# Small operations of the norms and of attention: other operands, other engines, and an identity added in four pieces

## The chip, the cores and the metric

The kernel runs on one core of one Trainium2 chip. The metric is the device time of one execution in microseconds (us). A core has five engines that each work through their own instructions in order: PE (TensorE, the matmuls; PEld is its weight load), DVE (VectorE), ACT (ScalarE), POOL (GpSimd) and SP (SyncE, here the queue that issues most DMAs). They wait for each other through semaphores only. SBUF is the large on-chip memory, PSUM the small one that the matmuls write.

## The reference, cut to what matters

Two layers work on x of shape (4, 512, 64, 64): 4 images of 512 channels and L = 4096 positions.

```
x = x + L0(gn(x))      # layer 0: layer norm, a Mamba scan over positions, layer norm, projection
x = x + L1(gn(x))      # layer 1: linear attention

gn(v): per image, 32 groups of 16 channels:  (v - mean) / sqrt(var + 1e-5)

L1:  q = relu(Wq x + bq);  k = relu(Wk x + bk);  v = Wv x + bv      # 8 heads of 64 channels
     kq   = sum over positions of k^T q                             # 64 x 64 a head
     attn = (v kq) / (kq.sum(axis=2) + 1e-6)
     out  = W_out attn + b_out
```

Three small pieces of this matter here. First, the statistics of `gn`: from the mean and the variance of each channel come the mean and the variance of each group, and from these a scale `gr` and an offset `off` for each channel. Secondly, kq is divided by its sum. Thirdly, layer 1 ends with `x + ...`, and the kernel folds that x into the last matrix by adding the identity to it.

## The kernel before, in words

Channels lie on partitions: 512 channels are NC = 4 blocks of P = 128. Positions are cut into NT = 8 tiles of T = 512. Layer 0 goes through 4 images x 8 tiles x 4 channel blocks = 128 steps (the list `steps`), each in SLOTS = 16 slots, so 2048 slots in all. In each slot the function `slot` issues

- on POOL, `drive`: one product `bx` of 128x1024 elements (L721), issued for the slot after next. `bx` has three buffers;
- on DVE, two scans `h` of 128x512 (L739), and in every second slot the product of `h` with `c_all` (L759, 128x1536);
- on ACT, two exponentials `dA` (L713) into three PSUM buffers, each released by a scan;
- on POOL, in every second slot, the copy `st` (L750) and the product of the last quarter of `h` with `c_sb` (L751);
- on PE, the matmuls that make `c_all` and those that sum `h` into `y`.

Then `slot` calls `after`, which issues everything else: the next steps' inputs, and the norms and layer 1 piece by piece. These pieces are Python generators in four queues: `ahead` (the norm of the next tile), `late` (the end of a tile in layer 0), `rest` (attention, that is layer 1) and `light` (the statistics of the next image). `one` takes one piece from a queue in a slot; whatever a generator issues between two `yield`s lies in that slot, behind the slot's scans on DVE. `later(1, f)` calls f in the next slot; `pause(1)` makes a generator go on in the next slot; `room` waits until few enough of the three PSUM work banks of `work_bank` are held, and `free` counts one back. So the order of each engine's instructions is written out by hand. Before the 2048 slots, and after them when only the attention of the last image is left, there are no slots (`now[0]` is None): `later` then calls at once, and `pause` does nothing.

The functions that the change touches:

- `stats_end` (L339 to L362) takes `mv`, the mean and variance of each channel (128x4 each), to `gr`, `off` and `ngm` (minus the group's mean). It copies the means to `cm` (L342), averages them over groups with a matmul with `grp` into the bank `pm`, copies that to `gm` (L347), forms the deviation and its square and adds the variance (L349 to L351), averages again (`pv`, in the same bank), adds the epsilon on DVE (L355), takes the power -1/2 on POOL (L357), and makes `ngm` and `off` on DVE (L360, L361). It runs twice an image: once for layer 0 (names ending in `_a`; from `input_norm`) and once for layer 1 (`_b`; from `attention`).
- `shifted` collects the sums for the second norm; for an image's first tile it takes a sample's statistics and sets `moff` (L554) and the first `square` (L556) on DVE.
- `shifted_end` (L567 to L576) turns these sums into `mv`: two reductions (L570), then on DVE a scaling (L571), `d2`, a subtraction and an addition (L573 to L575).
- `attention`, after kq is summed up: the reduction `nrm` (L898), + 1e-6 (L899), the reciprocal (L900), and two products of 64x256 into `kqn` (L903), which a POOL memset (L896) has zeroed. Then come the matmuls `pm` (twice), which fold the projections into one matrix `m3` (shown as `m` in the trace), and the matmuls `pob` for its offset `ob` (L951 on DVE). Last, 16 DVE additions of 32x32 (L976) put the identity onto `m3`'s diagonal, using `fold`, 32x32 identities stacked down the partitions. The matmuls `pr` then use `m3` for all 8 tiles, ACT adds `ob` (L979) and SP stores the result (L981).

All matmuls go through the helper `mm`, so every one of them has line L124.

Of the kernel before, what the change touches and what calls it, by code (L numbers as in the profile page):

```python
# [8 lines left out]
F32 = mybir.dt.float32  # L9
BF16 = mybir.dt.bfloat16  # L10
AF = mybir.ActivationFunctionType
ALU = mybir.AluOpType
AX = mybir.AxisListType

P = 128
T = 512
# [8 lines left out]
def kernel(  # L25
# [24 lines left out]
    nc = tc.nc  # L50
    B, C, L = x.shape
    NC = C // P
# [6 lines left out]
    BLK = 32  # L59
# [5 lines left out]
    small = ctx.enter_context(tc.tile_pool(name="small", bufs=2))  # L65
# [13 lines left out]
    def work_bank(name, behind=1):  # L79
        held[0] += behind  # L80
        return ps_w.tile([P, T], F32, tag="w", name=name)

    def free(n=1):
        held[0] -= n

    def later(n, what):

        done = []

        def both():  # L90
            what()
            done.append(True)

        if now[0] is None:
            both()
        else:
            due.append((now[0] + n, both))
        return done
# [5 lines left out]
    def until(*done):  # L104
        while not all(done):
            yield "wait"

    def pause(n):
        return until(later(n, lambda: None))

    def room(when="wait"):

        while now[0] is not None and held[0] >= limit[0]:
            yield when
# [6 lines left out]
    def mm(out_, lhsT, rhs, abreast=1, **how):  # L121

        work["mm"] += (0.25 if rhs.dtype == BF16 else 1.0) * rhs.shape[-1] / T / abreast
        nc.tensor.matmul(out_, lhsT, rhs, **how)  # L124
# [30 lines left out]
    def free_x():  # L155
        held_x[0] -= 1
# [17 lines left out]
    grp = const.tile([P, P // GROUP, GROUP], F32, tag="grp", name="grp")  # L174
# [9 lines left out]
    grp = grp.rearrange("p g i -> p (g i)")  # L184
# [4 lines left out]
    for i in range(1, 4):  # L189
        r = slice(i * LANE, (i + 1) * LANE)  # L190
# [10 lines left out]
    fold = const.tile([P, BLK], F32, tag="fold", name="fold")  # L201
    for k in range(KS):
        r = slice(k * BLK, (k + 1) * BLK)
# [47 lines left out]
    for e in range(NH):  # L251
        r = e * (LANE + NST)
# [30 lines left out]
    for i in (2, 3):  # L283
        r = slice(i * LANE, P)
# [16 lines left out]
    for o in range(NC):  # L301
        pw = work_bank(f"pw_{o}")
        for c in range(NC):
            mm(
                pw[:, 0:1], w_pr[:, c, o * P : (o + 1) * P], b_sb[:, c : c + 1],
                start=(c == 0), stop=(c == NC - 1),
# [13 lines left out]
    for c in range(NC):  # L320
        mm(
            pw[:, 0:1], ones.to_broadcast([P, P]), b_sb[:, c : c + 1],
            start=(c == 0), stop=(c == NC - 1),
# [8 lines left out]
    def aggregate(stats, name):  # L332

        mv = small.tile([P, NC, 2], F32, tag="mv", name=f"mv_{name}", bufs=4)
        for c in range(NC):
            nc.vector.bn_aggr(mv[:, c, :], stats[:, c, :, :].rearrange("p t s -> p (t s)"))
        return mv

    def stats_end(mv, name):  # L339

        cm = small.tile([P, NC], F32, tag="cm", name=f"cm_{name}")
        nc.vector.tensor_copy(cm, mv[:, :, 0])  # L342
        yield from room()
        pm = work_bank(f"pm_{name}")
        mm(pm[:, 0:NC], grp, cm, start=True, stop=True)
        gm = small.tile([P, NC], F32, tag="gm", name=f"gm_{name}")
        nc.vector.tensor_copy(gm, pm[:, 0:NC])  # L347
        dev = small.tile([P, NC], F32, tag="dev", name=f"dev_{name}")
        nc.vector.tensor_tensor(dev, cm, gm, ALU.subtract)  # L349
        nc.vector.tensor_tensor(dev, dev, dev, ALU.mult)  # L350
        nc.vector.tensor_tensor(dev, dev, mv[:, :, 1], ALU.add)  # L351
        pv = pm[:, NC : 2 * NC]
        mm(pv, grp, dev, start=True, stop=True)
        gr = small.tile([P, NC], F32, tag="gr", name=f"gr_{name}", bufs=4)
        nc.vector.tensor_scalar(gr, pv, 1e-5, None, ALU.add)  # L355
        free()
        nc.gpsimd.tensor_tensor(gr, gr, mhalf, ALU.pow)  # L357
        off = small.tile([P, NC], F32, tag="off", name=f"off_{name}", bufs=4)
        ngm = small.tile([P, NC], F32, tag="ngm", name=f"ngm_{name}", bufs=4)
        nc.vector.tensor_scalar(ngm, gm, -1.0, None, ALU.mult)  # L360
        nc.vector.tensor_tensor(off, ngm, gr, ALU.mult)  # L361
        return gr, off, ngm  # L362

    def group_norm(dst, xt, norm):
# [139 lines left out]
    def projected(ym, stats, x1, b, t):  # L504
# [27 lines left out]
        nc.gpsimd.dma_start(xt, cols(x, b)[:, :, t * T : (t + 1) * T], accum_op=ALU.add)  # L532
        yield from pause(4)
        yield from shifted(stats, xt, t, nm)
        nc.sync.dma_start(x1, xt)
        later(2, free_x)
# [9 lines left out]
    def shifted(f, xt, t, nm):  # L546
        if t == 0:
            for o in range(NC):
                nc.vector.bn_stats(f["first"][:, o, 0, :], xt[:, o, :])
                if o % 2:  # L550
                    yield
            f["mv"] = aggregate(f["first"], f"first_{nm}")
            f["off"] = small.tile([P, NC], F32, tag="moff", name=f"moff_{nm}")
            nc.vector.tensor_scalar(f["off"], f["mv"][:, :, 0], -1.0, None, ALU.mult)  # L554
            nc.vector.memset(f["sum"][:, :, 0:1], 0.0)
            nc.vector.tensor_scalar(f["square"][:, :, 0], f["mv"][:, :, 1], float(T), None, ALU.mult)  # L556
            return
        for o in range(NC):
            for v, func in (("sum", AF.Identity), ("square", AF.Square)):
                unused = wk.tile([P, T], F32, tag="res", name=f"{v}_{nm}_{o}", bufs=2)  # L560
                nc.scalar.activation(
                    unused, xt[:, o, :], func, bias=f["off"][:, o : o + 1],
                    accum_out=f[v][:, o, t : t + 1],
                )
            yield "free"

    def shifted_end(f, name):  # L567
        mv = small.tile([P, NC, 2], F32, tag="mv", name=f"mv_{name}", bufs=4)
        for v in range(2):
            nc.vector.tensor_reduce(mv[:, :, v], f[("sum", "square")[v]], AX.X, ALU.add)  # L570
        nc.vector.tensor_scalar(mv, mv, 1.0 / L, None, ALU.mult)  # L571
        d2 = small.tile([P, NC], F32, tag="d2", name=f"d2_{name}")
        nc.vector.tensor_tensor(d2, mv[:, :, 0], mv[:, :, 0], ALU.mult)  # L573
        nc.vector.tensor_tensor(mv[:, :, 1], mv[:, :, 1], d2, ALU.subtract)
        nc.vector.tensor_tensor(mv[:, :, 0], mv[:, :, 0], f["mv"][:, :, 0], ALU.add)  # L575
        return mv  # L576


# [227 lines left out]
    def attention(b, x1s, stats):  # L806
# [54 lines left out]
        for v in range(NT * SUB):  # L861
# [5 lines left out]
            for j in range(2):  # L867
# [4 lines left out]
                for c in range(NC):  # L872
                    mm(
                        pq, gn[:, c, u * P : (u + 1) * P], w_qk[:, c, j * C : (j + 1) * C],
                        start=False, stop=(c == NC - 1),
# [20 lines left out]
        nc.gpsimd.memset(kqn, 0.0)  # L896
        nrm = small.tile([P, NC], F32, tag="nrm", name=f"nrm_{b}")
        nc.vector.tensor_reduce(nrm, kq, AX.X, ALU.add)  # L898
        nc.vector.tensor_scalar(nrm, nrm, 1e-6, None, ALU.add)  # L899
        nc.vector.reciprocal(nrm, nrm)  # L900
        for i in range(P // HEAD):
            r = slice(i * HEAD, (i + 1) * HEAD)
            nc.vector.tensor_tensor(  # L903
                kqn[r, :, r], kq[r, :, :],
                nrm[r, :].unsqueeze(2).to_broadcast([HEAD, NC, HEAD]), ALU.mult,
            )
# [9 lines left out]
        for p in range(NC):  # L916
            yield from room()
            pm = work_bank(f"pm2_{b}_{p}")
# [6 lines left out]
        gr, _, ngm = norm  # L925
        m3 = wk.tile([P, NC, C], F32, tag="m3", name=f"m3_{b}", bufs=1)
# [6 lines left out]
        for m in range(NC):  # L933
            yield from room()
            pm = work_bank(f"pm3_{b}_{m}")
            for p in range(NC):
                mm(
                    pm, w_v[:, p, m * P : (m + 1) * P], m2[:, p, :],
                    start=(p == 0), stop=(p == NC - 1),
# [14 lines left out]
        for o in range(NC):  # L954
            yield from room()
            pm = work_bank(f"pob_{b}_{o}")
            for p in range(NC):
                mm(
                    pm[:, 0:1], m2[:, p, o * P : (o + 1) * P], bv[:, p : p + 1],
                    start=(p == 0), stop=False,  # L960
                )
            for m in range(NC):
                mm(
                    pm[:, 0:1], m3[:, m, o * P : (o + 1) * P], ngm[:, m : m + 1],
                    start=False, stop=(m == NC - 1),
# [3 lines left out]
        yield from until(*taken)  # L969
        free_x()  # L970
        free_x()
        for o in range(NC):
            for k in range(P // BLK):
                r = slice(k * BLK, (k + 1) * BLK)
                v = m3[r, o, o * P + k * BLK : o * P + (k + 1) * BLK]
                nc.vector.tensor_tensor(v, v, fold[r, :], ALU.add)  # L976
        def store(t, o, pp):
            res = wk.tile([P, T], F32, tag="res", name=f"res_{b}_{t}_{o}", bufs=2)
            nc.scalar.activation(res, pp, AF.Identity, bias=ob[:, o : o + 1])  # L979
            free()  # L980
            later(1, lambda: nc.sync.dma_start(cols(out, b)[:, o, t * T : (t + 1) * T], res))  # L981

        for t in range(NT):
            x1 = yield from fetched(t, "b")
            for o in range(NC):
                yield from room()
                pp = work_bank(f"pr_{b}_{t}_{o}")
                for m in range(NC):
                    mm(
                        pp, m3[:, m, o * P : (o + 1) * P], x1[:, m, :],  # L990
                        start=(m == 0), stop=(m == NC - 1),
# [39 lines left out]
    def leave(b, t):  # L1031
        if t == 0:
            stats1[b] = shifted_stats(b)
            x1s[b] = [
                dram.tile([P, NC, T], F32, tag="x1", name=f"x1_{b}_{i}", bufs=3 * NT)
                for i in range(NT)
            ]
        ym = xn[b, t][:, :, NTAP - 1 : NTAP - 1 + T]
        yield from projected(ym, stats1[b], x1s[b][t], b, t)
        if t == NT - 1:  # L1040
            add_to(rest, attention(b, x1s[b], stats1[b]))
# [52 lines left out]
    with tc.manual_schedule():  # L1094
        credit, seen, mix, held[0], held_x[0] = 0.0, work["mm"], iter(()), 0, 0
        for n, (b, t, c) in enumerate(steps):
            f, nm = fs[n], names[n]
# [142 lines left out]
```

## Time and profile before

| | us |
|---|---|
| median of 3 runs (lowest, highest) | 7940.75 (7933.85, 7962.12) |
| the profiled execution's own time | 7963.09 |
| its span, first to last instruction | 7961.4 |
| busy: DVE | 6977.7 (88% of the span) |
| busy: POOL | 6880.5 (86%) |
| busy: PE | 6453.6 (81%) |
| busy: ACT | 5507.6 (69%) |
| granted TensorE clock, mean | 0.897 |

Three stretches can be told apart by the busy time of the engines. Up to about 130 us the kernel sets up and takes the first statistics. From there to about 7400 us run most of the slots. From about 7500 us on only the attention of the fourth image is left: in the 461 us from 7500 to 7961, PE is busy for 425.2 us, DVE for 23.0 and POOL for 2.9.

A row of the groups of instructions gives the line, the engine, the operation, output<-inputs by the program's names, the shapes, and the count; then the busy time in us and the mean of one in ns; then the idle time of the engine just before these instructions in us, with what ended it. A line of the timeline gives start and duration in us, engine, line and operation, and in brackets the idle time before it with its releaser. The chain of waits is followed backwards from the last instruction: each of its pieces is a stretch of time which the end of the program waited for.

### The profile page before, as it was taken

To read this page: it belongs to the slowest core of one execution; us is meant where nothing else is said; L and a number is where in the kernel's file an instruction comes from. 1 tells how busy PE (TensorE), PEld (TensorE's weight loads), DVE (VectorE), ACT (ScalarE), POOL (GpSimd) and SP (SyncE) were. 2 spreads that over 40 slices of the span, in tenths; PEclk is the share of its full clock that TensorE was granted. 3 is DMA by queue.
4 is the path that set the end of the run, shared out by engine and by line. 5 is a ranking of instruction groups with operands and counts; after the bars stand their busy time and mean duration, and the time that the engine had idled before them with its cause. 6 is when DMAs were issued, how large, how long until landed. Compare 5 with 4: busy or idle time off the path is not lost.

```text
span 7961.4 us, 90563 instructions
## 1 busy us (share of the span) xinstructions
PE 6453.6 (81%) x24835; PEld 2120.0 (27%) x24880; DVE 6977.7 (88%) x5766; ACT 5507.6 (69%) x8321; POOL 6880.5 (86%) x4597
## 2 busy tenths in 40 slices
PE   5676777677789888888788888898688888888599
PEld 1121212112223222322222223332122332322144
DVE  5999999999999999989999999998999999988600
ACT  4667777777777777767777777677777777777421
POOL 4999999999999899989999899898999999889600
PEclk7888888888899999998899999899899999999799
DMA  5666666666666666777766666677666666676402
GB/s 154 167 168 166 151 155 159 160 155 167 169 179 162 151 163 159 174 189 175 174 155 171 171 157 161 155 185 189 156 167 163 161 161 159 145 194 180 112 32 90
DMA packets 829184, 1265.87 MB, mean 159 GB/s; under 512 B 183912, under 2 KB 317560, under 8 KB 816384
## 3 DMA queue, kind: packets, MB, share of 16 engines
q1 hardware_dynamic: 804736, 1222.32, 61.1%
q0 software_dynamic: 16896, 33.56, 2.4%
q10 hardware_dynamic: 7040, 4.20, 0.2%
q8 instruction: 195, 3.19, 0.2%
q14 instruction: 317, 2.60, 0.1%
HBM read 1052.78 MB, written 206.57 MB: 158 GB/s over the span
## 4 chain that ended last, share of the span: by engine, by line
DVE 33%; PE 21%; ACT 15%; DMA 12%; issue 8%; SPq 6%; POOL 6%; POOLq 0%; ACTq 0%; DVEq 0%
DVE h L739 22%; DVE h L759 9%; DMA d_all<-d_rows 7%; ACT dA L713 5%; PE pq L124 5%; POOL bx L721 4%; PE pc L124 4%; SPq L688 3%; PE y L124 3%; PE pr L124 3%; SPq L639 2%; DMA c_sb<-c_rows 2%; ACT xz L1048 2%; PE po L124 2%; ACT L1048 1%
## 5 line engine op out<-in xcount | busy, mean ns | idle before, releaser
L721 POOL TENSOR_TENSOR bx<-d_all,b_all 128x1024 f32<-128x1024 f32 x2048 | 4824.7, 2367 | 213.3 <-DVE h L739 195.1
L739 DVE TENSOR_TENSOR_SCAN h<-dA,st,bx 128x512 f32<-128x512 f32 x3584 | 4358.9, 1264 | 358.7 <-ACT dA L713 159.0
L713 ACT ACTIVATE dA<-d_all,a_t 128x512 f32<-128x512 f32 x4096 | 2752.9, 687 | 1568.5 <-DVE h L739 1521.8
L759 DVE TENSOR_TENSOR h<-h,c_all 128x1536 f32<-128x1536 f32 x1024 | 1767.5, 1726 | 0.1
L751 POOL TENSOR_TENSOR h<-h,c_sb 128x512 f32<-128x512 f32 x1024 | 1300.2, 1270 | 190.2 <-DMA c_sb<-c_rows 95.2
L124 PE MATMUL y<-h,fold 128*32 128x512 f32 x8192 | 1271.2, 696 | 71.6 <-POOL h L751 67.4
L124 PE MATMUL c_all<-parts,sel 128*128 128x384 bf16 x1024 | 369.9, 361 | 1123.3 <-DVE h L759 1121.7
L124 PE MATMUL pc<-xn,w_cv 128*128 128x512 f32 x2048 | 1045.7, 645 | 122.8 <-DVE xn L414 62.1
L124 PE MATMUL pq<-w_qk,xa 128*128 128x512 f32 x2048 | 965.5, 604 | 7.9 <-issue 5.3
L739 DVE TENSOR_TENSOR_SCAN h<-dA,bx 128x512 f32<-128x512 f32 x512 | 591.2, 1203 | 90.0 <-ACT dA L713 65.1
L124 PEld LDWEIGHTS <-sel 128*128 128x128 bf16 x1280 | 127.1, 99 | 1762.2 <-DVE h L759 1562.5
L124 PEld LDWEIGHTS pc<-xn,w_cv 128*128 128x128 f32 x2048 | 389.5, 201 | 747.1 <-issue 424.7
L124 PEld LDWEIGHTS pq<-w_qk,xa 128*128 128x128 f32 x2048 | 398.6, 196 | 439.6 <-issue 422.4
L124 PE MATMUL pr<-xb,m 128*128 128x512 f32 x1024 | 485.3, 612 | 7.5 <-DMA xb<-x 3.6
L124 PE MATMUL pp<-xn,w_pr 128*128 128x512 f32 x1024 | 477.7, 597 | 4.8 <-DVE xn L414 4.8
L124 PEld LDWEIGHTS y<-h,fold 128*32 128x32 f32 x8192 | 170.6, 114 | 644.0 <-issue 344.9
L124 PE MATMUL y<-xz,dg 32*32 32x512 f32 x2048 | 337.3, 734 | 0.0
L781 POOL TENSOR_TENSOR xz<-xz 128x512 f32<-128x512 f32 x256 | 325.7, 1272 | 9.2 <-ACT xz L778 9.2
L832 ACT ACTIVATE kq<-pq 128x512 f32<-128x512 f32 x256 | 150.5, 588 | 259.9 <-PE pq L124 259.2
L124 PE MATMUL pd<-xz,w_xp 128*128 128x512 f32 x512 | 323.4, 764 | 7.8 <-ACT xz L1048 7.8
L628 POOL TENSOR_TENSOR dt<-dt,xz 128x1024 f32<-128x1024 f32 x128 | 302.3, 2361 | 24.7 <-ACT dt L620 24.6
L124 PE MATMUL pz<-xn,w_z 128*128 128x512 f32 x512 | 275.4, 631 | 11.7 <-ACT xz L608 8.2
(179 smaller groups left out, 6034.1 us busy)
## 6 DMA issues: line engine op xcount, KB each, us to landing
d_all<-d_rows SPq DMA_DIRECT2D x2048, 256.0 KB, 6.7
b_all<-b_rows SPq DMA_DIRECT2D x4096, 64.0 KB, 2.2
d_rows<-dt SPq DMA_DIRECT2D x256, 512.0 KB, 3.6
c_sb<-c_rows SPq DMA_DIRECT2D x4096, 16.0 KB, 1.8
xs<-in_x_dram SPq DMA_DIRECT2D x32, 1024.0 KB, 6.3
xn<-in_x_dram SPq DMA_DIRECT2D x32, 1024.0 KB, 6.2
xr<-in_x_dram POOLq DMA_DIRECT2D x32, 1024.0 KB, 10.7
x<-xr SPq DMA_DIRECT2D x32, 1024.0 KB, 4.2
```

The source lines that it names most:

```text
L124: nc.tensor.matmul(out_, lhsT, rhs, **how)
L628: nc.gpsimd.tensor_tensor(f["both"][:, 1], f["both"][:, 0], f["xz"][:, 0], ALU.mult)
L639: nc.sync.dma_start(d[k * BLK : (k + 1) * BLK, v], src)
L688: nc.sync.dma_start(dst[k * BLK : (k + 1) * BLK, :], rows_[q * KS + k, :].partition_broadcast(BLK))
L713: nc.scalar.activation(dAs[k], fs[n]["d_all", e][:, 0, j, :], AF.Exp, scale=a_t[:, e, j, q : q + 1])
L721: nc.gpsimd.tensor_tensor(bxs[g], fs[n]["d_all", e][:, 1, jj * 2 : jj * 2 + 2, :], bc(b_all[g // JJ], 2), ALU.mult)
L739: nc.vector.tensor_tensor_scan(h[:, j, :], dAs.pop(2 * g + i), bxs[g][:, i, :], 0.0 if t == 0 else st[:, c, e, q, j : j + 1], ALU.mult, AL ...
L751: nc.gpsimd.tensor_tensor(h[:, :, CUT:], h[:, :, CUT:], bc(c_sb.pop(g // JJ), NJ), ALU.mult)
L759: nc.vector.tensor_tensor(own, own, bc(c_all.pop(g // JJ), NJ), ALU.mult)
L781: nc.gpsimd.tensor_tensor(f["xz"][:, 1, e, :], f["xz"][:, 1, e, :], f["xz"][:, 0, e, :], ALU.mult)
L832: nc.scalar.activation(qk[i], pq, AF.Relu)
L1048: nc.scalar.activation(fs[n]["xz"], fs[n]["xz"], AF.Silu)
```

## The change

In `stats_end`, the copies `cm` and `gm` go. The matmul reads `mv` directly. After it there is a `pause(1)`. Then `ngm` is made from the PSUM bank, the deviation is made twice on DVE, once into PSUM and once into SBUF, and their product (the square) and its sum with the variance each have one operand in PSUM. After the second matmul there is a second `pause(1)`. `off` is made on POOL.

In `shifted`, `moff` and the first `square` go to ACT. In `shifted_end`, the scaling and the three operations behind it go to POOL. In `attention`, the addition of 1e-6 and the two products `kqn` go to POOL, while the reciprocal stays on DVE. The identity is added on POOL with four instructions, each of which covers one 32x32 block in all four channel blocks (32x128 elements, the distance between blocks being C + P columns).

```diff
     def stats_end(mv, name):
-        cm = small.tile([P, NC], F32, tag="cm", name=f"cm_{name}")
-        nc.vector.tensor_copy(cm, mv[:, :, 0])
         yield from room()
         pm = work_bank(f"pm_{name}")
-        mm(pm[:, 0:NC], grp, cm, start=True, stop=True)
-        gm = small.tile([P, NC], F32, tag="gm", name=f"gm_{name}")
-        nc.vector.tensor_copy(gm, pm[:, 0:NC])
+        mm(pm[:, 0:NC], grp, mv[:, :, 0], start=True, stop=True)
+        yield from pause(1)
+        ngm = small.tile([P, NC], F32, tag="ngm", name=f"ngm_{name}", bufs=4)
+        nc.vector.tensor_scalar(ngm, pm[:, 0:NC], -1.0, None, ALU.mult)
+        d = pm[:, 2 * NC : 3 * NC]
+        nc.vector.tensor_tensor(d, mv[:, :, 0], pm[:, 0:NC], ALU.subtract)
         dev = small.tile([P, NC], F32, tag="dev", name=f"dev_{name}")
-        nc.vector.tensor_tensor(dev, cm, gm, ALU.subtract)
-        nc.vector.tensor_tensor(dev, dev, dev, ALU.mult)
-        nc.vector.tensor_tensor(dev, dev, mv[:, :, 1], ALU.add)
+        nc.vector.tensor_tensor(dev, mv[:, :, 0], pm[:, 0:NC], ALU.subtract)
+        nc.vector.tensor_tensor(d, dev, d, ALU.mult)
+        nc.vector.tensor_tensor(dev, d, mv[:, :, 1], ALU.add)
         pv = pm[:, NC : 2 * NC]
         mm(pv, grp, dev, start=True, stop=True)
+        yield from pause(1)
         gr = small.tile([P, NC], F32, tag="gr", name=f"gr_{name}", bufs=4)
         nc.vector.tensor_scalar(gr, pv, 1e-5, None, ALU.add)
         free()
         nc.gpsimd.tensor_tensor(gr, gr, mhalf, ALU.pow)
         off = small.tile([P, NC], F32, tag="off", name=f"off_{name}", bufs=4)
-        ngm = small.tile([P, NC], F32, tag="ngm", name=f"ngm_{name}", bufs=4)
-        nc.vector.tensor_scalar(ngm, gm, -1.0, None, ALU.mult)
-        nc.vector.tensor_tensor(off, ngm, gr, ALU.mult)
+        nc.gpsimd.tensor_tensor(off, ngm, gr, ALU.mult)
         return gr, off, ngm
...
     (in shifted)
-            nc.vector.tensor_scalar(f["off"], f["mv"][:, :, 0], -1.0, None, ALU.mult)
+            nc.scalar.activation(f["off"], f["mv"][:, :, 0], AF.Copy, scale=-1.0)
-            nc.vector.tensor_scalar(f["square"][:, :, 0], f["mv"][:, :, 1], float(T), None, ALU.mult)
+            nc.scalar.activation(f["square"][:, :, 0], f["mv"][:, :, 1], AF.Copy, scale=float(T))
...
     (in shifted_end)
-        nc.vector.tensor_scalar(mv, mv, 1.0 / L, None, ALU.mult)
+        nc.gpsimd.tensor_scalar(mv, mv, 1.0 / L, None, ALU.mult)
-        nc.vector.tensor_tensor(d2, mv[:, :, 0], mv[:, :, 0], ALU.mult)
-        nc.vector.tensor_tensor(mv[:, :, 1], mv[:, :, 1], d2, ALU.subtract)
-        nc.vector.tensor_tensor(mv[:, :, 0], mv[:, :, 0], f["mv"][:, :, 0], ALU.add)
+        nc.gpsimd.tensor_tensor(d2, mv[:, :, 0], mv[:, :, 0], ALU.mult)
+        nc.gpsimd.tensor_tensor(mv[:, :, 1], mv[:, :, 1], d2, ALU.subtract)
+        nc.gpsimd.tensor_tensor(mv[:, :, 0], mv[:, :, 0], f["mv"][:, :, 0], ALU.add)
...
     (in attention)
-        nc.vector.tensor_scalar(nrm, nrm, 1e-6, None, ALU.add)
+        nc.gpsimd.tensor_scalar(nrm, nrm, 1e-6, None, ALU.add)
         nc.vector.reciprocal(nrm, nrm)
         for i in range(P // HEAD):
             r = slice(i * HEAD, (i + 1) * HEAD)
-            nc.vector.tensor_tensor(
+            nc.gpsimd.tensor_tensor(
                 kqn[r, :, r], kq[r, :, :],
...
-        for o in range(NC):
-            for k in range(P // BLK):
-                r = slice(k * BLK, (k + 1) * BLK)
-                v = m3[r, o, o * P + k * BLK : o * P + (k + 1) * BLK]
-                nc.vector.tensor_tensor(v, v, fold[r, :], ALU.add)
+        for k in range(P // BLK):
+            r = slice(k * BLK, (k + 1) * BLK)
+            v = m3[r, 0, r]
+            v = bass.AP(v.tensor, v.offset, [v.ap[0], (C + P, NC), v.ap[1]])
+            nc.gpsimd.tensor_tensor(v, v, fold[r, :].unsqueeze(1).to_broadcast([BLK, NC, BLK]), ALU.add)
```

## The prediction

> **What bounds the kernel now.** I read the busy shares first, then the groups of instructions in the stretch from 130 to 7400 us (three images' worth of most changed lines, so x3), then the timelines of DVE and POOL around one changed piece, then the chain of waits through all of them. DVE (88%) and POOL (86%) are nearly level on the page, and in the 4000 us from 2000 to 6000 DVE is busy for 3728.5 us and POOL for 3681.1, 93% and 92%. Neither has much to spare, so the question is who waits for whom at the changed lines. DVE's groups:
>
> ```profile
> L361 DVE TENSOR_TENSOR off_a<-ngm_a,gr_a 128x4 f32<-128x4 f32 x3 | 6.9, 2308 | 3.2 <-POOL gr_a L357 3.2
> L361 DVE TENSOR_TENSOR off_b<-ngm_b,gr_b 128x4 f32<-128x4 f32 x3 | 6.9, 2302 | 3.2 <-POOL gr_b L357 3.2
> L573 DVE TENSOR_TENSOR d_b<-mv_b 128x4 f32<-128x4 f32 x3 | 6.7, 2243 | 0.1
> L903 DVE TENSOR_TENSOR kqn<-kq,nrm 64x256 f32<-64x256 f32 x6 | 6.5, 1077 | 0.5 <-POOL kqn L896 0.3
> L976 DVE TENSOR_TENSOR m<-m,fold 32x32 f32<-32x32 f32 x48 | 17.2, 358 | 0.6
> L351 DVE TENSOR_TENSOR dev_b<-dev_b,mv_b 128x4 f32<-128x4 f32 x3 | 0.5, 163 | 0.1
> L839 DVE TENSOR_TENSOR kq<-pk,kq 128x256 f32<-128x256 f32 x93 | 37.4, 402 | 17.1 <-PE pk L124 16.9
> ```
>
> Four elements a partition take 2.3 us in `off` and `d_b` but 0.16 us in `dev_b`. The timeline of the second image's event shows why; first DVE, then POOL:
>
> ```profile
> 3959.26 2.24 DVE L573 TENSOR_TENSOR d_b<-mv_b 128x4 f32<-128x4 f32 x1
> 3963.52 0.16 DVE L347 COPY gm_b<-pm_b 128x4 f32<-128x4 f32 x1 [0.54 <-PE pm_b L124]
> 3966.07 2.30 DVE L361 TENSOR_TENSOR off_b<-ngm_b,gr_b 128x4 f32<-128x4 f32 x1 [1.08 <-POOL gr_b L357]
> 3968.30 1.21 DVE L739 TENSOR_TENSOR_SCAN h<-dA,bx 128x512 f32<-128x512 f32 x1
> ```
>
> ```profile
> 3956.81 4.67 POOL L721 TENSOR_TENSOR bx<-d_all,b_all 128x1024 f32<-128x1024 f32 x2
> 3964.99 1.04 POOL L357 TENSOR_TENSOR gr_b<-gr_b,mhalf 128x4 f32<-128x4 f32 x1 [2.04 <-DVE ngm_b L360]
> 3966.02 2.33 POOL L721 TENSOR_TENSOR bx<-d_all,b_all 128x1024 f32<-128x1024 f32 x1
> 3972.36 2.36 POOL L721 TENSOR_TENSOR bx<-d_all,b_all 128x1024 f32<-128x1024 f32 x1 [4.02 <-DVE h L739]
> ```
>
> `off_b` begins 0.05 us after a `bx` and ends with it (3968.37 against 3968.35); `d_b` ends at 3961.50, with the `bx` at 3961.48. So the small operation lasts as long as POOL's large one. Meanwhile POOL runs out of `bx` buffers and idles: 2.04 + 4.02 us here. The chain of waits runs straight through:
>
> ```profile
> 3959.26 2.25 DVE d_b L573
> 3961.81 1.18 DVE cm_b L342
> 3965.00 1.05 POOL gr_b L357
> 3966.07 2.30 DVE off_b L361
> 3968.37 1.13 DVE h L739
> ```
>
> At these places DVE bounds the kernel, and POOL is the one that waits.
>
> **What the Trainium skill says.** "SBUF — State Buffer", section "Who interferes with whom", says that a Vector instruction with two SBUF inputs, or a copy or tensor_scalar in a two-port mode, takes turns with GpSimd on a port, and the later one waits for the whole of the other; a reduction never does. The trace agrees: 2.3 us beside `bx`, and 0.16 to 0.17 us for the reductions of L570, though a `bx` runs then too. "VectorE: DVE Perf Modes", section "Why PSUM operands drop a tier", says that a PSUM operand shuts an instruction out of the two-port modes. What I need, that an instruction with one PSUM operand keeps clear of POOL, shows in `kq<-pk,kq`: one input in PSUM, one in SBUF, 93 times amid POOL's work, mean 402 ns for 256 elements. "GPSIMD Engine Reference", section "3.1 Elementwise — side-by-side cycle accounting", puts a two-input operation at about twice DVE's time; here `bx` takes 2367 ns for 1024 elements and the product of L751 1270 ns for 512.
>
> **The change, part by part.** Durations are from the stretch 130 to 7400 us, three images, unless said otherwise.
>
> *DVE, taken away.* `stats_end`: both `off` with their waits 2 x (6.9 + 3.2) = 20.2; both `cm` 1.6 + 3.5 = 5.1; both `gm` 1.0 with their waits for PE 10.8 + 1.6; the two waits before `gr` 1.4 + 1.4, which the pauses put behind a slot of scans: 41.5 us. Added is one subtraction in each of six calls, 6 x 0.16 = 1.0. `shifted_end`: 1.7 + 6.7 + 0.5 + 0.5 = 9.4. `nrm` and `kqn`: 3.6 + 6.5 + 0.5 = 10.6. The identity: 17.2 + 0.6 = 17.8. `moff` and `square` (four images): 4.4 + 2.8 = 7.2. Sum 85.5 us, the most that DVE can gain.
>
> *How much lies on the path.* I went through the chain of waits at each event. The three calls for layer 0 stand on it for 5.0, 5.1 and 5.0 us (from `pm` to the end of `off`; the long wait before is PE's own queue, which the change leaves). The three for layer 1: 5.1, 9.5 and 9.5. `nrm` with `kqn`: 3.8, 3.0 and 2.5. The identity: 5.3, 5.2 and 7.2. `moff` and `square`: under 0.2 together. Sum 66.2. Of this stay six DVE operations of 0.16 to 0.2 us in each `stats_end`, 6 x 1.1 = 6.6, two pairs of reductions 0.4, and a hand-over DVE to POOL to DVE for `nrm`, which I take at 0.7 us each, 2.1. So 57 us leave the chain.
>
> *What is late next.* ACT, PE and SP are held back by the same scans (ACT idles 9.89 us before its `dA` at 3969.54), but the chain elsewhere leaves DVE for transfers of `d_all`, for ACT's tables and for PE; such a side path may already have been within a few us. I let 80% of 57 come through: 46 us. Of the 28 us that DVE gains off the chain I count a quarter, 7 us, as cover where scans are late afterwards.
>
> *POOL, added.* From 2367 and 1270 ns follow 2.14 ns an element and 173 ns fixed. Per image: `off` twice, `nrm` and three small steps of `shifted_end`, 6 x 0.18; its scaling 0.19; `kqn` 2 x 0.72; the identity 4 x 0.45. Sum 4.5 us, 13.5 for three images. The small ones are bounded by the copy `st`, 0.20 (no gain is possible, POOL had none of this work), and by the power of the same 128x4, 1.04; I take 0.18, and with 1.04 it is 10.5 an image, 31 us in all. POOL's idle time around these events (at layer 0's norms 3.8, 10.9, 9.3; at layer 1's 3 x 6.0; at `kqn` 5.1, 5.1, 3.9; at the identity 5.4, 5.4, 6.6) is 73 us, so at 13.5 it is nearly all hidden. I count 3 us. If that idle time were not there, it would cost the full 13.5.
>
> *Waits added.* POOL's scaling waits for DVE's reductions, its `nrm` for DVE's sum, its identity for PE's last `pob`. Behind each stand the next `bx`, and behind those the scans. POOL is up to two slots ahead (three buffers), so such a wait eats its lead, up to a slot of 3.6 us (7270 us for 2019 of `bx`), before it delays a scan. The reciprocal on DVE now waits for POOL (counted above). The bank `pm` is held two slots longer, and the third bank taken after it waits on PE; the row `gm` shows 0.5 to 5.2 us of such PE lateness. Between 0 and 3.6 us in six calls; I take 0.5, 3 us.
>
> *ACT* gets two operations of four elements in each image; "ScalarE: Activation LUTs", section "What ACT_TABLE_LOAD costs", prices such an instruction with fixed scale at 186 ns, so 8 x 0.19 = 1.5 us, beside an ACT that is busy for 69%. Nothing.
>
> *Start and end without slots.* There no POOL work competes, and each small DVE operation takes 0.16 to 0.19. `off` on POOL costs nothing at the start. At the end four `shifted_end` steps on POOL take 0.7 against 0.67, plus a hand-over of 0.2; `nrm` and `kqn` 0.18 + 1.44 plus three hand-overs of 0.2 against 0.17 + 0.85, so +1.2; the identity comes wholly behind the last `pob` (4 x 0.45 plus 0.3), where before `pr` began at 7844.18 right after it, so +2.1. Less `cm`, 0.3. Sum +3.5, say 4.
>
> *Sum:* -46 - 7 + 3 + 3 + 4 = -43 us. Against the profiled execution 7963.1 that is 7920; it lies 22 us above the median, and I carry the difference over: 7940.75 - 43 = 7898.
>
> **The rivals.** *A, the time is given back:* the chain moves to side paths. For it speaks that DVE holds only 33% of the whole chain, and transfers, SP and ACT a third; against it that all of them stand idle at the events. With a third of the 57 us: -19, -2 or so off the chain, + 10: about -11, 7930. *B, POOL becomes the bound:* at 92% it has little air. Each of three waits an image costs a slot, 3 x 3 x 3.6 = 32, its work 13.5, and DVE's gain ends in waits for `bx`: 7941 + 45 = 7986. It decides from the point where POOL's 73 us of idle time is not the cover I take it for; then waits of the scan for `bx` (now 77 us in this stretch) grow by as much. Against it: POOL idles right after each event for want of buffers. *C, all of it counts:* 66 - 7 on the chain and most of the rest: -79, 7862. *D, an operand in PSUM does not keep DVE clear of POOL:* then `stats_end` keeps four waits of 2.3 x 6, up to 55, and the result is +12, 7953; `kq<-pk,kq` speaks against it.
>
> **How the numbers follow.** About 0.5% (40 us) is what a measurement of this kernel can tell from no change. My forecast, -25 to -65, has 62%; it straddles the border at -40, 36 of it below and 26 above. A 20% (same), B 5% (slower), C 10% (faster), D 3% (same). Faster 0.46, same 0.49, slower 0.05. The range goes from C's 7862 to just under D, 7948.
>
> **What would show it.** Right: `off`, `d2`, `kqn` and the identity gone from DVE; `ngm` to `gr` at about 0.16 us each though POOL runs; no wait for `pm`; POOL's bx-waits on DVE at the events gone; small POOL operations at 0.2, `kqn` at 0.7. Wrong: POOL's small operations at 1 us, the scan's waits for `bx` up by tens of us, or DVE's busy time down by 70 us and the span not.

## The result, and the profile after

| | before | after |
|---|---|---|
| median of 7 runs, us | 7947.32 | 7905.43 |
| lowest to highest, us | 7933.85 to 7965.76 | 7896.7 to 7924.96 |
| ratio, 95% interval | | 0.9945 [0.9933, 0.9957] |
| profiled execution: own time, us | 7963.09 | 7900.44 |

The change saves about 44 us by the ratio [34, 53], 42 by the medians; the forecast was 43. The two profiled executions differ by more, 63 us, because that of before lies 16 us above its median and that of after 5 below; so the traces below are read for single waits and durations, and sums are held against the ratio.

One rival of the whole account was not named before: the granted TensorE clock. Over the seven runs of the changed kernel it was 0.902 on average, over the 71 runs of the kernel before that were made along with the experiments 0.898. Among those 71, compared on one chip, a run with 0.001 more was 3 us shorter on average. If the clock were a cause and not a companion of shorter waits, that would be, as an estimate, 13 of the 44 us. Most of the gain is not the clock's: the run b1 below gained 40 us at 0.899. Which of the two drives the other no run shows.

The page of after, busy time by engine:

```profile
PE 6434.6 (81%) x24834; PEld 2109.1 (27%) x24880; DVE 6908.9 (87%) x5650; ACT 5509.8 (70%) x8329; POOL 6894.4 (87%) x4649
```

DVE lost 69 us of busy time, POOL gained 14. DVE's groups of after, stretch 130 to 7400 us (count 3: three images):

```profile
L346 DVE TENSOR_SCALAR ngm_b<-pm_b 128x4 f32<-128x4 f32 x3 | 0.5, 162 | 3.7 <-PE pm_b L124 3.7
L350 DVE TENSOR_TENSOR dev_b<-mv_b,pm_b 128x4 f32<-128x4 f32 x3 | 0.5, 158 | 0.1
L900 DVE RECIPROCAL nrm<-nrm 128x4 f32<-128x4 f32 x3 | 0.5, 178 | 3.3 <-POOL nrm L899 3.3
```

and POOL's:

```profile
L976 POOL TENSOR_TENSOR m<-m,fold 32x128 f32<-32x128 f32 x12 | 5.4, 446 | 3.8 <-PE pob L124 3.3
L903 POOL TENSOR_TENSOR kqn<-kq,nrm 64x256 f32<-64x256 f32 x6 | 3.6, 608 | 1.1 <-DVE nrm L900 0.6 <-DMA d_rows<-dt 0.3
```

Of the four-element operations that `stats_end`, `shifted_end` and `attention` still have on DVE, no group's mean is above 0.18 us. That this is not because POOL happens to rest is seen in the timeline of the first image's call for layer 1 (some lines of it), DVE ahead of POOL:

```profile
2084.99 0.16 DVE L346 TENSOR_SCALAR ngm_b<-pm_b 128x4 f32<-128x4 f32 x1 [1.29 <-PE pm_b L124]
2085.07 0.16 DVE L348 TENSOR_TENSOR pm_b<-mv_b,pm_b 128x4 f32<-128x4 f32 x1
2085.26 0.16 DVE L350 TENSOR_TENSOR dev_b<-mv_b,pm_b 128x4 f32<-128x4 f32 x1
2085.73 2.33 DVE L739 TENSOR_TENSOR_SCAN h<-dA,bx 128x512 f32<-128x512 f32 x2
```

```profile
2084.46 4.67 POOL L721 TENSOR_TENSOR bx<-d_all,b_all 128x1024 f32<-128x1024 f32 x2
2092.92 0.20 POOL L361 TENSOR_TENSOR off_b<-ngm_b,gr_b 128x4 f32<-128x4 f32 x1
```

All of these small DVE operations run inside POOL's pair of `bx` (2084.46 to 2089.13) and still take 0.16 us, each with one operand in PSUM, and the scan follows at once. `off_b` comes 7 us later, and in the stretch from 130 to 7330 us no engine is seen to wait for it.

### The profile page after: what moved, and what is told of

Its sections match the earlier page's. It is cut to its first block, busy times and chain, and to the rows that moved or that the text cites. A ratio compares the mean times of both kernels' runs of the same rounds, so it can differ in the third digit from the quotient of the medians.

```text
span 7898.7 us, 90490 instructions
## 1 busy us (share of the span) xinstructions
PE 6434.6 (81%) x24834; PEld 2109.1 (27%) x24880; DVE 6908.9 (87%) x5650; ACT 5509.8 (70%) x8329; POOL 6894.4 (87%) x4649
## 4 chain that ended last, share of the span: by engine, by line
DVE 32%; PE 21%; DMA 13%; ACT 12%; issue 8%; POOL 7%; SPq 6%; POOLq 0%; DVEq 0%; ACTq 0%
DVE h L739 22%; DVE h L759 9%; DMA d_all<-d_rows 7%; PE pq L124 5%; POOL bx L721 5%; ACT dA L713 4%; PE pc L124 4%; SPq L688 3%; PE y L124 3%; PE pr L124 2%; SPq L639 2%; PE po L124 2%; DMA c_sb<-c_rows 2%; ACT xz L1049 2%; DMA b_all<-b_rows 2%
```

## The experiments

My theory was that of the prediction: small DVE operations on SBUF operands sat on the path because they waited out POOL's products, and about 60% of DVE's 85 us would reach the end. Rival 1: the waits for PE, which the two pauses take away, are the gain. Rival 2: POOL is the bound, or close to it. Each ratio is to the kernel before, on the same chip; "us" is the ratio's distance from 1 times 7945. Not all rows come from one chip, and a difference between two rows carries the errors of both.

| kernel | ratio [95%] | us |
|---|---|---|
| changed kernel | 0.9945 [0.9933, 0.9957] | -44 |
| p1: stats_end alone | 0.9966 [0.9953, 0.9979] | -27 |
| p2: identity alone | 0.9994 [0.9987, 1.0002] | -5 |
| p3: the other moves alone | 0.9996 [0.9988, 1.0003] | -3 |
| p4: the pauses alone | 1.0009 [1.0002, 1.0017] | +7 |
| a1: changed, without pauses | 0.9959 [0.9946, 0.9973] | -33 |
| a2: changed, SBUF operands in stats_end | 0.9962 [0.9949, 0.9974] | -30 |
| a4: changed, identity as before | 0.9957 [0.9944, 0.9969] | -34 |
| d1: changed, +84 us of DVE | 0.9996 [0.9987, 1.0004] | -3 |
| d2: changed, +97 us of POOL at slot 12 | 0.9939 [0.9927, 0.9952] | -48 |
| d3: changed, +97 us of POOL at slot 4 | 0.9963 [0.9951, 0.9975] | -29 |
| d4: changed, a small SBUF operation a step | 0.9966 [0.9952, 0.9979] | -27 |
| b1: changed, later reads | 0.9950 [0.9938, 0.9962] | -40 |

**The parts (p1, p2, p3).** Each puts one part of the change's diff onto the kernel before: p1 the new `stats_end`, p2 the last hunk, p3 the hunks in between.

> The kernel before with only the new stats_end (PSUM operands, two pauses, off on GpSimd). My theory, that VectorE's small operations stood on the path because they waited out GpSimd's products: 27 us leave the chain, 80% of it and a quarter of the 13 us off the chain come through, less 4 for GpSimd's off and the longer held bank: about -21 us. Rival 1, the waits for TensorE that the pauses take away are the gain: about as much here, but then the pauses alone show it too. Rival 2, GpSimd is the bound: near 0.

> The kernel before with only the identity added on GpSimd in four operations an image. My theory: 17.7 us on the chain, 80% through, less 1 for GpSimd's 5.4 us and 2 at the end without slots: about -11 us. Rival 1 (pauses): 0. Rival 2 (GpSimd is the bound): +5 or more.

> The kernel before with the other moves only: moff and square to ScalarE, shifted_end, the addition of 1e-6 and kqn to GpSimd. My theory: 12.6 us net on the chain, 80% through, a quarter of 14.6 off the chain, less 3.5 for GpSimd's work and the end without slots: about -10 us. Rival 1: 0. Rival 2: +5 or more.

`stats_end` carries most of it, -27 [-37, -17], and rival 2 is not seen in any part. The identity (-5) and the other moves (-3) gave less than forecast, and neither can be told from no change alone. For p3 the trace shows a reason. DVE's waits, stretch 130 to 7330 us (total, times, longest):

```profile
DVE cm_b L342 <- POOL mv_b L575: 15.9, 3, 5.8
```

With `shifted_end` on POOL, but with the old `stats_end` behind it, DVE's very next operation, the copy `cm`, needs what POOL makes, and POOL is in the middle of its products: DVE stands for 15.9 us in three images, more than the 9.4 us that moving `shifted_end` freed. In the changed kernel there is no `cm`; a matmul and a pause stand between, and what is left of the wait is 3.7 us in three (`ngm_b` above). For the identity no such reason was found; nor was it tried whether four instructions on DVE would do as well as four on POOL.

**The pauses (p4, a1).**

```diff
         mm(pm[:, 0:NC], grp, ..., start=True, stop=True)
+        yield from pause(1)          # p4: into the kernel before;  a1: out of the changed one
...
         mm(pv, grp, dev, start=True, stop=True)
+        yield from pause(1)
```

> The kernel before with the two pauses in stats_end only; all operations stay where they are and as they are. Rival 1 (VectorE's waits for TensorE, 15 us in the 130 to 7400 us stretch, were the gain): -10 to -15 us. My theory: the pauses move the operations of stats_end into slots in which GpSimd is in the middle of a product, so more of them wait: dev (two operations with both operands in SBUF) and the copy of cm at up to 2.3 us each, so between -5 and +20 us.

> The changed kernel without its two pauses in stats_end. My theory: VectorE waits for TensorE again, 15 us in all of which some 8 lie on the path: -34 us against the kernel before. Rival 1 (the pauses are the gain): -25 us or less of the gain left, that is, most of stats_end's part gone.

Rival 1 falls: alone, the pauses cost 7 us [2, 14]. The groups of p4 show what they do when the operands stay in SBUF:

```profile
L350 DVE TENSOR_TENSOR dev_b<-cm_b,gm_b 128x4 f32<-128x4 f32 x3 | 7.1, 2360 | 0.1
L363 DVE TENSOR_TENSOR off_b<-ngm_b,gr_b 128x4 f32<-128x4 f32 x3 | 6.9, 2301 | 11.2 <-POOL gr_b L359 11.2
```

In the kernel before the same `dev_b`, also with SBUF operands, took 0.16 us, since POOL was standing at its own wait for `gr`:

```profile
L349 DVE TENSOR_TENSOR dev_b<-cm_b,gm_b 128x4 f32<-128x4 f32 x3 | 0.5, 161 | 0.1
```

One slot later it meets a `bx` and takes 2.36. The timeline of p4, first image, shows the meeting, POOL's line and then DVE's:

```profile
2097.42 2.35 POOL L723 TENSOR_TENSOR bx<-d_all,b_all 128x1024 f32<-128x1024 f32 x1 [1.70 <-DVE gm_b L348]
2097.43 2.36 DVE L350 TENSOR_TENSOR dev_b<-cm_b,gm_b 128x4 f32<-128x4 f32 x1
```

The scan in front (2096.13 to 2097.34) gave POOL its buffer back; one DVE operation, `gm`, slipped in ahead, and the next came 0.01 us behind the start of `bx`. And DVE, which still makes `off`, waits 11.2 us for the power that POOL now reaches later. In the changed kernel the pauses have a use: without them (a1) the estimate is 11 us worse, though the two intervals overlap, and DVE again waits for the matmul, which waits for POOL:

```profile
DVE ngm_b L345 <- PE pm_b L124: 17.3, 3, 6.2
```

**The operands (a2).**

```diff
+        cm = small.tile(...);  nc.vector.tensor_copy(cm, mv[:, :, 0])
         yield from room()
-        mm(pm[:, 0:NC], grp, mv[:, :, 0], start=True, stop=True)
+        mm(pm[:, 0:NC], grp, cm, start=True, stop=True)
         yield from pause(1)
...
+        # gm, dev, its square and the sum as in the kernel before; off stays on POOL
```

> The changed kernel, but stats_end copies the means to SBUF first and works on SBUF operands as before; the pauses and off on GpSimd stay. My theory: cm, the difference dev, its square and the sum wait out GpSimd's product where one runs: up to 4 x 2.3 us in each of six calls, if half of them meet one 28 us, of which 80% reach the end: -20 us against the kernel before. Theory D (an operand in PSUM does not matter): the same as the changed kernel, -42.

-30 against -44, with overlapping intervals, so the time alone does not settle it. Nor would the time belong to the operands alone: with `cm` back, DVE waits for POOL's `mv` again, as in p3. The durations tell what the operands do. In a2's groups:

```profile
L350 DVE TENSOR_TENSOR dev_b<-cm_b,gm_b 128x4 f32<-128x4 f32 x3 | 7.1, 2363 | 0.1
L342 DVE COPY cm_b<-mv_b 128x4 f32<-128x4 f32 x3 | 6.8, 2280 | 18.1 <-POOL mv_b L577 18.1
```

The same subtraction at the same place takes 2.36 us with both inputs in SBUF and 0.16 with one in PSUM. Not each of the four operations pays: in the calls for layer 1 it is `cm` (2.28) and `dev_b`, while the square and the sum behind `dev_b` took 0.16, since by then the product had ended (in p4 at 2099.77, the square began at 2099.82) and POOL was waiting for the next scan. That is why 4 x 2.3 was too high a bound.

So the operands in PSUM are no gain over the kernel before by themselves, where the subtraction took 0.16 us too; they keep the pauses from costing what they cost in p4. How the 27 us of p1 divide was not tried. By the prediction's count `off` with its wait is 20.2 of the 41.5 us that `stats_end` takes from DVE, and the kernel before with `off` alone on POOL was not run.

**How much of an engine's time reaches the end (d1, d2, d3).**

```diff
                     if s >= 12:
                         next(mix, None)
+                    if s == 12:                  # d3: s == 4
+                        nc.vector.tensor_reduce(spare, w_pr[:, 0, :], AX.X, ALU.add)              # d1
+                        for _ in range(3):                                                        # d2, d3
+                            nc.gpsimd.tensor_tensor(spare, grp[:, 0:BLK], grp[:, BLK : 2 * BLK], ALU.mult)
```

> The changed kernel with one more VectorE operation in each of the 128 steps: a reduction of 512 SBUF elements, about 0.69 us, 88 us in all, whose result nobody uses. It measures how much of VectorE's time reaches the end. My prediction's share of 80% for work on the path: +70 us against the changed kernel, +28 against the kernel before. With VectorE's share in the chain (a third) as the measure: +29 against the changed kernel.

> The changed kernel with three more GpSimd operations in each of the 128 steps: products of 32 elements, about 0.24 us each, 92 us in all, whose result nobody uses. My prediction counted 3 of 13.5 us of GpSimd's new work: +20 us against the changed kernel. Rival 2 (GpSimd is the bound): +80 to +92.

> The changed kernel with three more GpSimd operations of 32 elements in each step, as in the run at slot 12 (97 us in all, which cost nothing there), but at slot 4, right behind the step's large product for dt, where GpSimd has most to do. If GpSimd has room everywhere: within 10 us of the changed kernel. If it bounds the stretch around slot 4: +40 to +97 us.

The added DVE reductions took 0.66 us (median), 84 us in all, and cost some 41 us: a share of 48% (35 to 62% with the errors of both rows), between the two figures that were named. The added POOL products took 0.25 us, 97 us in all, and cost nothing that can be seen at slot 12 (-48 against -44, where 20 us more had been expected) and about 14 us at slot 4, where the intervals still overlap. Rival 2 falls: an engine that is busy for 87% took 97 us more for 0 to 14 us of time. POOL's waits, stretch 130 to 7330 us, before, after, d1 and d2:

```profile
POOL bx L721 <- DVE h L739: 194.6, 287, 6.6
POOL h L751 <- DMA c_sb<-c_rows: 93.5, 61, 6.6
```

```profile
POOL bx L721 <- DVE h L739: 139.9, 227, 3.6
POOL h L751 <- DMA c_sb<-c_rows: 123.3, 80, 5.7
```

```profile
POOL bx L722 <- DVE h L740: 156.9, 274, 3.6
POOL h L752 <- DMA c_sb<-c_rows: 90.9, 60, 5.5
```

```profile
POOL bx L722 <- DVE h L740: 84.7, 110, 4.1
POOL h L752 <- DMA c_sb<-c_rows: 79.3, 53, 5.3
```

With DVE relieved, POOL waits 55 us less for buffers but 30 us more for `c_sb`, a transfer that the change leaves as it was (1.8 us from issue to landing, median, before and after); with DVE loaded again (d1) the wait for `c_sb` is back at 91. With more work on POOL (d2) the work fills these waits: the two rows fall by 99 us. So a part of what DVE gains turns up in waits for this transfer. That it is the larger part of what does not arrive was not tried.

**A small SBUF operation by itself (d4).**

```diff
+                    if s == 12:
+                        nc.vector.tensor_tensor(spare, g_sb, b_sb, ALU.mult)       # spare: 128x4
```

> The changed kernel with one more VectorE operation of four elements a partition in each of the 128 steps, both inputs in SBUF, the result unused. If such an operation waits out GpSimd's product: mean 1 to 2.3 us each, 130 to 290 us of VectorE time, half of which reaches the end (the share that the longer reductions showed): +65 to +145 us against the changed kernel. If its 0.16 us were all it costs: 20 us of VectorE time, +10.

This missed both figures. In the stretch of 130 to 7330 us:

```profile
L1155 DVE TENSOR_TENSOR spare<-g_sb,b_sb 128x4 f32<-128x4 f32 x126 | 43.1, 342 | 0.0
```

The median of all 128 is 0.136 us, the longest 2.17, and 98 took less than 0.2. At this slot POOL is mostly standing still, waiting for the scan in front of this very operation to give its buffer back:

```profile
POOL bx L722 <- DVE h L740: 95.8, 164, 4.3
POOL bx L722 <- DVE spare L1155: 63.9, 90, 3.6
```

90 times a `bx` is put down to this operation's end, behind the scan that frees its buffer: the small operation went first. The price was paid where POOL's product had begun: each of the 30 longer ones started while a `bx` ran and ended within 0.03 us of its end, and 91 of the 98 short ones started with no POOL operation running. It cost 17 us, overlapping intervals again, for the 43 us of DVE time; that is 40%, which cannot be told from d1's 48%.

**An attempt at more (b1).**

```diff
-            taken.append(later(1, lambda o=o, pm=pm: offset(o, pm)))
+            taken.append(later(2, lambda o=o, pm=pm: offset(o, pm)))
...
-            return later(soon(), lambda: add(pk, v == 0))
+            return later(soon() + 1, lambda: add(pk, v == 0))
```

> The changed kernel with VectorE's reads of pob one slot later and its additions to kq one slot later, which takes away the 7 and 19 us that VectorE waits there for TensorE. If half of that reaches the end: -13 us against the changed kernel. The work banks are held a slot longer, which may take it back: then 0 or a few us slower.

No gain: -40. Both waits are all but gone (0.3 us is left before `ob`), but DVE's scans now wait longer for PE and for POOL (90.6 and 89.4 us in the changed kernel):

```profile
DVE h L739 <- PE y L124: 118.8, 110, 6.6
DVE h L739 <- POOL bx L721: 102.6, 82, 6.6
```

28 and 13 us more, no less than was taken away, and the reciprocal's wait for POOL grew from 3.3 to 8.8 us. So no version here is faster than the changed kernel by more than the noise.

**Parts together (a4).**

> The changed kernel with the 16 VectorE additions of the identity put back, that is, stats_end and the other moves together. Alone they gave -27 and -3. Theory of the hidden wait: alone, the other moves lose 16 us to VectorE's copy cm, which waits until GpSimd has made mv; with the new stats_end that wait lies behind a matmul and a pause, so together they give more than -30, about -37 against the kernel before. Theory of plain sums: -30.

-34 [-45, -25] lies between -30 and -37; that cannot decide whether the parts help each other. The three parts alone add up to -35, the whole gave -44, within the intervals. That p3's wait goes away with the new `stats_end` is shown by the rows above, not by this time.

## Why the prediction came out right

- *What bounds the kernel at these places: DVE, by waiting out POOL.* Right. `dev_b` at 2.36 us with SBUF operands (p4, a2) and 0.16 with PSUM (p1, changed kernel), beside a running `bx`, shows it; rival D falls with it. One reading was wrong, without harm: of POOL's 2.04 + 4.02 us in the example, the 2.04 is its wait for the input of `gr` (the line has `ngm_b` as releaser), and only the 4.02 a want of `bx` buffers.
- *85 us of DVE, 53 us of it to the end (80% of 57 on the chain, a quarter of 28 beside it).* The sum held: the slots end 47 to 49 us earlier if the 5 us that the end lost are added to the 42 to 44 measured; the prediction, its 6 us for POOL and for added waits taken off the 53, had 47. As a share of DVE's 85.5 us that is 55 to 57% measured and 55% predicted (62% before the 6 us), and 48% for d1's time spread over all steps. That about half comes through is shown by d1; that the sum came within 1 us, with an interval of [34, 53], is luck. The 80% and the quarter by themselves were choices, and no run shows them singly.
- *The split.* Off in both directions: `stats_end` -27 for a forecast of -21, identity -5 for -11, the rest -3 for -10. The first forecast lies within the measured interval, the other two at the far edges of theirs (-10 both). Alone the parts add up to -35 for -42, so that the whole came out at -44 is again not owed to the split. What the identity lacked is not settled; for the rest the trace shows a reason, the wait of `cm` for POOL, which belongs to a mixture of old and new code and not to the changed kernel; what this wait costs at the end was not measured.
- *POOL, 3 us of 13.5.* The work was sized nearly right: `kqn` 0.61 us where 0.72 was worked out, the identity 0.45 for 0.45, small ones 0.20 to 0.25 (the scaling `mv`) for 0.18 and 0.19, far from the upper end of 1.04. Its cost at the end is between none (d2) and 14% of it (d3), so 0 to 2 us as an estimate. The scan's waits for `bx`, whose growth by tens of us was to speak for rival B, went from 77.4 to 89.4 us.
- *Waits added.* The reciprocal waits 3.3 us in three images (2.1 counted). The wait for `pm`, which was to be gone, is 5.3 us (12.4 before); 3.7 of it is at layer 1, where the matmul now waits for `mv` from POOL. A wait for the work bank was not tried by itself.
- *The end without slots: +4.* From the first reduction to the last instruction it takes 416.1 us (7482.6 to 7898.7) against 411.3 (7550.1 to 7961.4). 2.2 of the 4.8 us is PE's wait for the identity, as worked out; 2.3 is more busy time of PE (399.8 against 397.6), which was not foreseen (1.7 of it in the eight matmuls that read `kqn`, 5.40 us against 3.67; why was not looked into); PE's wait for `kqn` grew by 0.2 where I had 1.2. PE's wait on the trace of after:

```profile
7780.94 1.95 POOL L976 TENSOR_TENSOR m<-m,fold 32x128 f32<-32x128 f32 x4 [30.22 <-PE pob L124]
7782.94 2.07 PE L124 MATMUL pr<-xb,m 128*128 128x512 f32 x2 [2.18 <-POOL m L976]
```

- *Rival A* (a third gets through, -11 us) and *B* (POOL, +45) are both out: the result's interval is -53 to -34 us, and POOL took seven times the added work at little or no cost.

## What to carry to other kernels

Look for tiny operations with long durations: compare one shape across lines, and where 0.16 us turns into 2.3, look at what the other engine has running. Moving such an operation to the engine it waits for can pay even though that engine is just as busy, and one operand in PSUM kept it at 0.16 us here in all six calls; but a value that goes to the other engine and comes straight back makes its reader wait for what is queued there (15.9 us in three calls of p3), unless a slot lies between. Take a busy share of 87% as no proof of a bound: ask what the engine's idle time waits for, and price a us on each engine by adding some.

## What the runs showed of the hardware that was not expected

- The wait between DVE and POOL depended on who started first, and 0.01 us (`dev_b` in p4) or 0.05 us (`off_b`) behind the start of a `bx` was enough for the whole of it. `off`, released by the end of POOL's power, met the start of POOL's next `bx` in six of six calls with slots (2.30 us each); the same kind of operation right behind the scan that POOL waits for mostly went first (98 of 128 under 0.2 us).
- A POOL product of 64 partitions by 256 elements took 0.608 us, under the 0.72 that 128 partitions' rows give; 32 by 128 took 0.446, no less than those rows give.
- On ACT the two moved operations of 128x4 took 0.20 and 0.19 us (medians).
